# Layer 3's softmax sums as block sums on VectorE in seven of eight images, image 6's output products by halves between image 7's units, and the next image's residual sums behind the last transpose

## The chip, the cores and the metric

The kernel runs on one core of one Trainium2 chip. Its time is the device time of one execution in microseconds (us). Engines: TensorE (PE) multiplies matrices, VectorE (DVE) and ScalarE (ACT) work on elements, GpSimd (POOL) does some additions, SyncE (SP) issues most DMAs. Each engine takes its instructions in a fixed order and waits at an instruction until its operands are there.

## The reference

Eight images of 384 channels and 32 x 32 positions pass four residual layers, x = x + layer(normalised x): layer 0 an attention with convolved queries, keys and values, layer 1 a mixture of four experts per position, layer 2 a 3 x 3 depthwise and a 1 x 1 convolution with ternary weights, layer 3 an attention with keys and values sampled at 256 learned points. All is float32. The change is in the end of layer 3:

```
attn = jax.nn.softmax(jnp.einsum('bhqd,bhkd->bhqk', qh, k) * SCALE, axis=-1)   # 6 heads, 1024 queries, 256 keys, 64 wide
out = jnp.einsum('bhqk,bhkd->bhqd', attn, v)
out = out.transpose(0, 1, 3, 2).reshape(B, DIM, H, W)
out = jnp.einsum('bchw,oc->bohw', out, proj_w) + proj_b[None, :, None, None]
```

## The kernel before

A tile holds one image as 128 partitions x 3 chunks x 1024 positions. Layers 0 and the first pass of layer 1 fill the first half of the time. After that a loop goes over the images: the generator `layers(b)` gives layers 2 and 3 of image b in small steps, and between two steps units of layer 1 of image b + 1 (`layer1`, its matmuls into `ph` at L1492 and `y` at L1513) are put in, so that PE has work while DVE does the convolution of layer 2 (`y<-h,tap,y`, L1632). From this a scheduler makes one fixed order for each engine. Image 7 has no image after it: `last_image` takes what is left of image 6's generator by `fill(n)`, n steps at a time, and puts it between its own steps.

`attend` is the attention of layer 3. It has six units u, one for each pair of heads pr (0 to 2) and half of the queries h (0, 1). A unit is:

- scores: four matmuls into two tiles `s`, each of the two-bank tag `big`, of which there are two (L1867);
- ACT takes the exponentials of both into two tiles `p` (L1884), and POOL adds the two into `p01` (L1953);
- four matmuls of `p` with the values into `pav`, of a bank of its own (L1893), which DVE transposes by 32 x 32 blocks into `tu` (L1965);
- the sum of the exponentials over the keys, in one of two ways. `sums` (L1906): two matmuls of `ones` with `p01` into `pss`, 64 columns of PE each, and DVE transposes the 128 x 512 result into `ts` (L1938). Or `block_sums` and `join`: DVE transposes `p01` by blocks (`tp`, L1917, 128 x 1024) and adds over each block's 32 (`bsum`, L1919), and two matmuls with 16 columns of operand add up the partitions into `pbs` (L1926);
- `divide`, one unit later: DVE takes the reciprocal (L1935 or L1939), multiplies `tu` by it (L1940) and transposes into the slice of `att` that belongs to pr and h (L1943).

`blocks` says how many units take the second way: units 0 to 3 of images 0 to 5, none of images 6 and 7. After the units come the output products: for each of three row blocks m, six matmuls `pf<-att,wp` into one `big` tile (halves h, and pr within a half, L2022), and DVE adds bias and x (L2030) and a DMA takes the result out.

`layer1(b + 1)` begins with `attended`: three DVE instructions `x<-o,bnsc_out,x` of 128 x 1024 (L1226), one for each chunk, then ACT's `h` (L1442), which the first `ph` needs. In the order of before they stand on DVE among the divisions of image b's units 4 and 5. After the output products the two small matmuls `gna_d` and `gnb_d` (L117, L128) give the norm with which layer 2 of the next image starts.

Of the kernel before, what the change touches and what calls it, by code (L numbers as in the profile page):

```python
# [9 lines left out]
ALU = mybir.AluOpType  # L10
AX = mybir.AxisListType

B, C, H, W = 8, 384, 32, 32
N = H * W
P = 128
# [40 lines left out]
def tile_kernel(ctx: ExitStack, tc: tile.TileContext, i: dict, out: bass.AP):  # L56
# [1344 lines left out]

    x2_dram = dram.tile([B, P, KC, N], F32, name="x2")
    om_dram = dram.tile([B, 3, NG * LS], F32, name="omd")
    NU3, NB3 = 2 * NPAIR3, 4
    rec3 = wd.tile([P, B * NU3, 16], F32, name="rec3")
    bad3 = wd.tile([P, 1], mybir.dt.int32, name="bad3")

# [7 lines left out]
    def layer1(pl, b, late=False):  # L1415
# [13 lines left out]
        def enter(h):  # L1429
            hs = slice(h * HALF, (h + 1) * HALF)  # L1430
            if late and h == 1:

                h1 = [pl.one([P, HALF], t, f"h1_{b}_{t}", n) for t, n in (("cb", 2), ("w0", 1))]
                h1.insert(0, pl.one([P, HALF], "cb", f"h1_{b}", 2))
            else:
                h1 = pl.one([P, KC, HALF], "h1", f"h1_{b}_{h}")
                h1 = [h1[:, c, :] for c in range(KC)]
            state["h1"] = h1
            if h == 0 and not late:
                attended(xt, ots)  # L1440
            for c in range(KC):
                nc.scalar.activation(  # L1442
                    h1[c], xt[:, c, hs], AF.Identity,
                    bias=sb1[:, b, c : c + 1], scale=rs1[:, b : b + 1],
                )
# [385 lines left out]
    def attend(pl, b, xt, put, general, q, xs, fill=nothing):  # L1831
# [69 lines left out]
        if not general:  # L1901
            def sums(u, p01):

                pss = fbank(f"pss3_{b}_{u}")
                for j in range(2):
                    nc.tensor.matmul(  # L1906
                        pss[64 * j : 64 * j + 64, :], lhsT=ones[:, :64],
                        rhs=p01[:, j * HALF : (j + 1) * HALF], start=True, stop=True,
                    )
                return pss  # L1910

            blocks = NB3 if b < B - 2 else 0

            def block_sums(u, p01):

                t = pl.one([P, 32, 32], "ts", f"tp_{b}_{u}")
                nc.vector.transpose(t.rearrange("p a b -> p (a b)"), p01)  # L1917
                bsum = small.tile([P, 32], F32, tag="bsum", name=f"bsum_{b}_{u}")
                nc.vector.reduce_sum(bsum, t, AX.X)  # L1919
                return bsum  # L1920

            def join(u, bsum):

                pss = fbank(f"pbs3_{b}_{u}")
                for j in range(2):
                    nc.tensor.matmul(  # L1926
                        pss[64 * j : 64 * j + 64, :16], lhsT=same,
                        rhs=bsum[:, 16 * j : 16 * j + 16], start=True, stop=True,
                    )
                return pss  # L1930

            def divide(pss, pr, h, u, tu):
                rc = rec3[:, b * NU3 + u, :]
                if u < blocks:
                    nc.vector.reciprocal(rc, pss[:, :16])  # L1935
                else:
                    tss = pl.one([P, 16, 32], "ts", f"ts_{b}_{u}")
                    nc.vector.transpose(tss.rearrange("p a b -> p (a b)"), pss)  # L1938
                    nc.vector.reciprocal(rc, tss[:, :, 0])  # L1939
                nc.vector.tensor_tensor(  # L1940
                    tu, tu, rc.unsqueeze(2).to_broadcast([P, 16, 32]), ALU.mult
                )
                nc.vector.transpose(  # L1943
                    att[:, pr, h * HALF : (h + 1) * HALF], tu.rearrange("p a b -> p (a b)")
                )


            ps, due3 = exps(0, scores(*units[0])), None
            fill(1)
            yield UNIT  # L1950
            for u, (pr, h) in enumerate(units):
                p01 = pl.flat([P, N], f"p01_{b}_{u}")
                nc.gpsimd.tensor_tensor(p01, ps[0], ps[1], ALU.add)  # L1953
                nxt = scores(*units[u + 1]) if u + 1 < NU3 else None
                if last and nxt:
                    nxt = exps(u + 1, nxt)
                pav = weigh(pr, h, ps)
                if due3:
                    pss = (join if due3[2] < blocks else sums)(due3[2], due3[4])
                if nxt:  # L1960
                    ps = nxt if last else exps(u + 1, nxt)

                tu = pl.one([P, NG * LS], f"om{u % 2}", f"tu_{b}_{u}")[:, :HALF]
                tu = tu.rearrange("p (a b) -> p a b", b=32)
                nc.vector.transpose(tu.rearrange("p a b -> p (a b)"), pav)  # L1965
                if due3:
                    divide(pss, *due3[:4])
                due3 = pr, h, u, tu, block_sums(u, p01) if u < blocks else p01
                if u < KC:
                    fill(1)  # L1970
                yield UNIT
                yield 0.0
            divide(sums(due3[2], due3[4]), *due3[:4])
            yield 3.0
        else:
            for pr, h in units:
                pav = vbank(f"pav3_{b}_{pr}_{h}")
                for j in range(2):
                    r = slice(64 * j, 64 * j + 64)
                    nm = f"3_{b}_{pr}_{h}_{j}"  # L1980
                    s = big(f"s{nm}").rearrange("p (a k) -> p a k", a=4)
                    for qc in range(4):
                        q0 = h * HALF + qc * P
                        nc.tensor.matmul(
                            s[:, qc, :], lhsT=q[r, pr, q0 : q0 + P], rhs=kt[r, pr, :],
                            start=True, stop=True,
                        )
                    mx = small.tile([P, 4], F32, tag="mx4", name=f"mx{nm}")
                    nc.vector.reduce_max(mx, s, AX.X, negate=True)
                    nc.vector.tensor_scalar(mx, mx, 0.125, None, ALU.mult)  # L1990
                    p = pl.flat([P, 4, LS], f"p{nm}")
                    rs = small.tile([P, 4], F32, tag="rs4", name=f"rs{nm}")
                    for qc in range(4):
                        nc.scalar.activation(
                            p[:, qc, :], s[:, qc, :], AF.Exp, bias=mx[:, qc : qc + 1],
                            scale=0.125, accum_out=rs[:, qc : qc + 1],
                        )
                    nc.vector.reciprocal(rs, rs)
                    nc.vector.tensor_tensor(
                        p, p, rs.unsqueeze(2).to_broadcast([P, 4, LS]), ALU.mult  # L2000
                    )
                    pt = pl.flat([P, 2, HALF], f"pt{nm}")
                    for kc in range(2):
                        tp = fbank(f"tp{nm}_{kc}")
                        for qc in range(4):
                            nc.tensor.transpose(
                                tp[:, qc * P : (qc + 1) * P], p[:, qc, kc * P : (kc + 1) * P], ident
                            )
                        nc.vector.tensor_copy(pt[:, kc, :], tp)
                    hd = 2 * pr + j  # L2010
                    for kc in range(2):
                        nc.tensor.matmul(
                            pav[r, :], lhsT=vt[:, kc, hd * 64 : (hd + 1) * 64], rhs=pt[:, kc, :],
                            start=(kc == 0), stop=(kc == 1),
                        )
                nc.vector.tensor_copy(att[:, pr, h * HALF : (h + 1) * HALF], pav)
        for m in range(KC):
            pf = big(f"pf_{b}_{m}")
            for h in range(2):
                hs = slice(h * HALF, (h + 1) * HALF)  # L2020
                for pr in range(NPAIR3):
                    nc.tensor.matmul(  # L2022
                        pf[:, hs], lhsT=wp3[:, pr, m * P : (m + 1) * P], rhs=att[:, pr, hs],
                        start=(pr == 0), stop=(pr == NPAIR3 - 1),
                    )

            n = 2 if last and m == KC - 1 else 1
            for k in range(n):
                ks = slice(k * N // n, (k + 1) * N // n)
                nc.vector.scalar_tensor_tensor(  # L2030
                    xt[:, m, ks], pf[:, ks], pb3[:, m : m + 1], xt[:, m, ks], ALU.add, ALU.add
                )
                put(m, xt, ks)
            yield 0.0

    oks = wd.tile([P, 2], F32, name="oks")
# [138 lines left out]
    with pd:  # L2175
# [30 lines left out]
        def fill(n):  # L2206
            for _ in range(n):
                next(this, None)
# [173 lines left out]
```

## Time and profile before

| what | value |
|---|---|
| median of 3 runs | 3445.78 us (3443.03 to 3448.07) |
| the profiled execution | 3446.12 us, span of its trace 3444.3 us |
| granted clock of PE | 0.99 |
| PE, DVE, ACT, POOL busy | 97%, 51%, 38%, 6% of the span |
| DMA over the span | 68 GB/s in the mean |

The span runs from the first to the last instruction; the execution is 1.8 us longer. A float32 matmul stands in the trace as two records, so 36 records of `pf` are 18 matmuls.

### The profile page before, as it was taken

The page shows a single profiled execution, that of the slowest core. Times are in us where ns is not written, and L with a number is a line of the kernel's source. Part 1 is how long each engine was busy: PE and PEld are TensorE (multiplying, and loading weights), DVE is VectorE, ACT ScalarE, POOL GpSimd, SP SyncE. Part 2 cuts the span into 40 slices and gives each one's busy share as a digit, 9 for nine tenths or more (in the row PEclk, how much of TensorE's full clock was granted, in tenths as well). Part 3 has the DMA queues.
Part 4 walks back from the last instruction along what each step waited for, and adds up shares of the span by engine and source line. Part 5 has one row for each costly group of instructions (what it writes and reads, how often), then busy time and mean ns, then how long its engine had stood idle before and what let it go on. Part 6 is the DMA issues. An engine that isn't in the chain of part 4 may idle for free.

```text
span 3444.3 us, 44805 instructions
## 1 busy us (share of the span) xinstructions
PE 3338.8 (97%) x18479; PEld 1445.0 (42%) x18479; DVE 1754.6 (51%) x2961; ACT 1300.2 (38%) x1519; POOL 203.7 (6%) x237
## 2 busy tenths in 40 slices
PE   6989999999999999998889999999999999999988
PEld 2433434343434343433334444444444444444443
DVE  8952232323232323234456575565755657548764
ACT  5655444444444444433212323223232232322341
POOL 2100000000000000000000100101001010020121
PEclk9999999999999999999999999999999999999999
DMA  9973121212121212021810110101101001010000
GB/s 354 295 222 80 27 80 27 80 27 80 26 81 26 80 27 79 28 75 44 309 35 22 36 46 30 55 22 36 42 33 55 22 36 40 36 55 22 0 19 38
DMA packets 86547, 234.56 MB, mean 68 GB/s; under 512 B 21832, under 2 KB 22056, under 8 KB 79418
## 3 DMA queue, kind: packets, MB, share of 16 engines
q1 hardware_dynamic: 84170, 223.30, 20.1%
q10 hardware_dynamic: 1248, 4.72, 0.4%
q8 instruction: 149, 2.44, 0.3%
q0 software_dynamic: 912, 3.53, 0.3%
q14 instruction: 68, 0.56, 0.1%
HBM read 146.33 MB, written 75.59 MB: 64 GB/s over the span
## 4 chain that ended last, share of the span: by engine, by line
PE 43%; DVE 7%; ACT 1%; DMA 1%; POOL 0%; issue 0%; SPq 0%; DVEq 0%; POOLq 0%; ACTq 0%
PE y L1513 12%; PE ph L1492 11%; DVE y L1632 4%; PE pf L2022 4%; PE pq L1673 3%; PE pw L1644 3%; PE pav L1893 3%; PE s L1867 2%; PE pk L1838 1%; DVE hd L1478 1%; DVE off L1769 1%; PE pv L1849 1%; PE pss L1906 1%; PE xsb L1819 1%; PE pw_last L2071 1%; PE xs L1819 0%
## 5 line engine op out<-in xcount | busy, mean ns | idle before, releaser
L827 ACT ACTIVATE p<-s 128x1024 f32<-128x1024 f32 x512 | 496.3, 1021 | 365.7 <-PE s L820 365.5
L1492 PE MATMUL ph<-h,w_sb 128*128 128x512 f32 x1104 | 487.2, 596 | 14.7 <-DMA b_sb<-in_b_dram 14.5
L1513 PE MATMUL y<-hd,w_sb 128*128 128x512 f32 x1080 | 487.2, 599 | 10.8 <-DVE hd L1478 10.8
L835 PE MATMUL pav<-p,vt 64*64 64x512 f32 x4096 | 494.8, 589 | 0.0
L820 PE MATMUL s<-qk,qk 48*64 48x512 f32 x2944 | 355.2, 592 | 0.0
L1492 PEld LDWEIGHTS ph<-h,w_sb 128*128 128x128 f32 x1104 | 208.1, 191 | 272.0 <-issue 265.4
L1513 PEld LDWEIGHTS y<-hd,w_sb 128*128 128x128 f32 x1080 | 200.0, 191 | 242.1 <-issue 220.3
L796 DVE COPY ta<-pav 128x512 f32<-128x512 f32 (+1 forms) x65 | 44.2, 681 | 475.2 <-PE pav L835 475.2
L835 PEld LDWEIGHTS pav<-p,vt 64*64 64x64 f32 x4096 | 168.4, 133 | 273.6 <-issue 273.3
L1502 ACT ACTIVATE hd<-ph,b_sb 128x512 f32<-128x512 f32 x180 | 122.7, 682 | 308.4 <-PE ph L1492 308.4
L574 PE MATMUL pk<-xs,cws_sb 32*32 32x496 f32 (+3 forms) x3840 | 179.3, 605 | 40.5 <-DMA xs<-in_xs_dram 24.6
L1769 DVE SCALAR_TENSOR_TENSOR off<-q,dw_sb,off 128x225 f32<-128x225 f32 (+4 forms) x441 | 215.3, 542 | 2.6
L1632 DVE SCALAR_TENSOR_TENSOR y<-h,tap,y 128x961 f32<-128x961 f32 (+1 forms) x168 | 202.8, 1227 | 0.5
L820 PEld LDWEIGHTS s<-qk,qk 48*64 48x64 f32 x2944 | 109.4, 133 | 211.2 <-issue 190.3
L81 DVE COPY qk<-pq 128x512 f32<-128x512 f32 x46 | 31.8, 691 | 251.9 <-PE pq L258 251.9
L1884 ACT ACTIVATE p<-s 128x1024 f32<-128x1024 f32 x96 | 93.7, 1021 | 170.8 <-PE s L1867 161.4
L1478 DVE TENSOR_TENSOR hd<-hd,cb 128x512 f32<-128x512 f32 x180 | 122.2, 684 | 37.7 <-ACT hd L1502 37.5
L574 PEld LDWEIGHTS pk<-xs,cws_sb 32*32 32x32 f32 (+1 forms) x3840 | 80.3, 111 | 137.9 <-issue 49.2
L1953 POOL TENSOR_TENSOR p<-p,p 128x1024 f32<-128x1024 f32 x48 | 113.6, 2367 | 335.3 <-ACT p L1884 306.4
L820 PE MATMUL s<-ql,ql 48*64 48x512 f32 x1024 | 128.3, 592 | 0.2 <-ACT p L827 0.2
L2022 PE MATMUL pf<-att,wp_sb 128*128 128x512 f32 x288 | 127.4, 596 | 0.0
L711 PE MATMUL pv<-wv_sb,g 128*128 128x384 f32 x384 | 127.1, 489 | 0.0
(369 smaller groups left out, 3748.6 us busy)
## 6 DMA issues: line engine op xcount, KB each, us to landing
rqk<-y SPq DMA_DIRECT2D x96, 256.0 KB
g<-rqk SPq DMA_DIRECT2D x96, 256.0 KB
xs<-in_xs_dram SPq DMA_DIRECT2D x56, 384.0 KB
g<-rv SPq DMA_DIRECT2D x48, 256.0 KB
xh<-in_x_dram SPq DMA_DIRECT2D x48, 256.0 KB
f<-in_x_dram SPq DMA_DIRECT2D x24, 512.0 KB
f<-o SPq DMA_DIRECT2D x24, 512.0 KB
o<-ot SPq DMA_DIRECT2D x42, 256.0 KB
```

Source lines behind the costliest of these rows:

```text
L574: nc.tensor.matmul(banks[r][cols[q]].rearrange("p (h w) -> p h w", w=W)[:, :, c0:c1], lhsT=cws[rs, c, 2 * h + g, x, w], rhs=src[rs, :, c0 ...
L711: nc.tensor.matmul(pv[:, :C], lhsT=acts[b][2][:, c, t * P : (t + 1) * P], rhs=w_in[2][:, c, :], start=(c == 0), stop=(c == KC - 1),)
L820: nc.tensor.matmul(s[64 * k : 64 * k + 64, j * HALF : (j + 1) * HALF], lhsT=kt[r, k0 : k0 + 64], rhs=qt[r, h * HALF : (h + 1) * HALF], sta ...
L827: nc.scalar.activation(p, s, AF.Exp, scale=scale)
L835: nc.tensor.matmul(pav[k][64 * j : 64 * j + 64, :], lhsT=vts[b % 2][r, kc, 2 * hd : 2 * hd + 2, :].rearrange("p a b -> p (a b)"), rhs=p[r, ...
L1478: nc.vector.tensor_tensor(hd, hd, state["cb"], ALU.mult)
L1492: ahead["ph"] = nc.tensor.matmul(ph, lhsT=w1[:, e, c, dc * P : (dc + 1) * P], rhs=state["h1"][c], start=(c == 0), stop=(c == KC - 1),)
L1502: nc.scalar.activation(hd, ph, AF.Relu, bias=b1[:, k : k + 1])
L1513: nc.tensor.matmul(y, lhsT=w2[:, e, dc, m * P : (m + 1) * P], rhs=state[h, k], start=(k == 0), stop=(k == NE * KC - 1),)
L1632: nc.vector.scalar_tensor_tensor(d, f, tap2[:, c, t : t + 1], d, ALU.mult, ALU.add)
L1769: nc.vector.scalar_tensor_tensor(d, f, dw3[:, t : t + 1], d, ALU.mult, ALU.add)
L2022: nc.tensor.matmul(pf[:, hs], lhsT=wp3[:, pr, m * P : (m + 1) * P], rhs=att[:, pr, hs], start=(pr == 0), stop=(pr == NPAIR3 - 1),)
```

## The change

Images 0 to 5 and 7 take block sums for all six units (`joined = b != B - 2`); image 6 keeps the matmuls with `ones` for all of its units. Image 6's output products go by halves: three matmuls into one bank of the tag `f` (three banks, shared with the small sums), an addition of 128 x 512 and a DMA for each half, and a step of the generator behind each; `last_image` calls `fill(1)` in every one of image 7's units, not in the first three alone. `attended` of the next image is issued after the last transpose into `att`.

```diff
-    NU3, NB3 = 2 * NPAIR3, 4
+    NU3 = 2 * NPAIR3
...
             if h == 0 and not late:
-                attended(xt, ots)
+                with tc.issue_after(ahead["att"].ins) if "att" in ahead else nullcontext():
+                    attended(xt, ots)
...
-            blocks = NB3 if b < B - 2 else 0
+            joined = b != B - 2
...
-                if u < blocks:
+                if joined:
                     nc.vector.reciprocal(rc, pss[:, :16])
...
-                nc.vector.transpose(
+                ahead["att"] = nc.vector.transpose(
                     att[:, pr, h * HALF : (h + 1) * HALF], tu.rearrange("p a b -> p (a b)")
                 )
...
-                    pss = (join if due3[2] < blocks else sums)(due3[2], due3[4])
+                    pss = (join if joined else sums)(due3[2], due3[4])
...
-                due3 = pr, h, u, tu, block_sums(u, p01) if u < blocks else p01
-                if u < KC:
-                    fill(1)
+                due3 = pr, h, u, tu, block_sums(u, p01) if joined else p01
+                fill(1)
                 yield UNIT
                 yield 0.0
-            divide(sums(due3[2], due3[4]), *due3[:4])
+            divide((join if joined else sums)(due3[2], due3[4]), *due3[:4])
...
+        halves = [slice(h * HALF, (h + 1) * HALF) for h in range(2)]
+
+        def output(pf, m, hs):
+
+            for pr in range(NPAIR3):
+                nc.tensor.matmul(
+                    pf, lhsT=wp3[:, pr, m * P : (m + 1) * P], rhs=att[:, pr, hs],
+                    start=(pr == 0), stop=(pr == NPAIR3 - 1),
+                )
+
+        def add(pf, m, ks):
+            nc.vector.scalar_tensor_tensor(
+                xt[:, m, ks], pf, pb3[:, m : m + 1], xt[:, m, ks], ALU.add, ALU.add
+            )
+            put(m, xt, ks)
+
         for m in range(KC):
+            if b == B - 2:
+                for h, hs in enumerate(halves):
+                    pf = fbank(f"pf_{b}_{m}_{h}")
+                    output(pf, m, hs)
+                    add(pf, m, hs)
+                    yield 0.0
+                continue
             pf = big(f"pf_{b}_{m}")
...
+            for hs in halves:
+                output(pf[:, hs], m, hs)
+            for ks in halves if last and m == KC - 1 else [slice(0, N)]:
+                add(pf[:, ks], m, ks)
             yield 0.0
```

What the schedulers make of it, in each engine's order. On PE, at the end of images 0 to 5: `pav` of unit 4, `pbs` of units 3 and 4, one matmul of `pf`, `pav` of unit 5, five of `pf`, `pbs` of unit 5, six of `pf`, one of the next image's `ph`, six of `pf`, two of `ph`, `gna_d`. On DVE there: `tu` of unit 4, both reciprocals, both products, both transposes into `att`, `tu`, `tp` and `bsum` of unit 5, its division, two of the three sums of `attended`, two of `x<-pf`, then the third sum. On PE in image 7: in each unit three matmuls of image 6's `pf` where six stood in units 0 to 2, and `pbs` where `pss` stood. On SP the one difference is that image 6 goes out in six DMAs of 256 KB, not three of 512 KB.

More of the change, by code (lines that the diff above doesn't have):

```diff
@@ L2016, in attend @@
                 nc.vector.tensor_copy(att[:, pr, h * HALF : (h + 1) * HALF], pav)
-        for m in range(KC):
-            pf = big(f"pf_{b}_{m}")
[L2019 to L2033, printed above, removed]
+        halves = [slice(h * HALF, (h + 1) * HALF) for h in range(2)]
[10 more added lines that the diff above has]
+            put(m, xt, ks)
+        for m in range(KC):
+            if b == B - 2:
[5 more added lines that the diff above has]
+                continue
+            pf = big(f"pf_{b}_{m}")
+            for hs in halves:
+                output(pf[:, hs], m, hs)
+            for ks in halves if last and m == KC - 1 else [slice(0, N)]:
+                add(pf[:, ks], m, ks)
             yield 0.0
```

## The prediction

> **What bounds the kernel.** First the page's busy times:
>
> ```profile
> PE 3338.8 (97%) x18479; PEld 1445.0 (42%) x18479; DVE 1754.6 (51%) x2961; ACT 1300.2 (38%) x1519; POOL 203.7 (6%) x237
> ```
>
> PE hardly ever stands, at a granted clock of 0.99, so what counts is PE's own work and the waits that PE meets. Next the chain of waits at a junction, the end of image 4's attention:
>
> ```profile
> 2854.11 1.87 PE pav L1893 x8
> 2855.98 0.07 PE pbs L1926 x4
> 2856.06 0.89 PE pss L1906 x2
> 2856.95 1.88 PE pav L1893 x8
> 2858.83 1.72 PE pss L1906 x6
> 2860.55 3.63 PE pf L2022 x8
> 2864.18 1.72 PE ph L1492 x4
> 2865.89 12.02 PE pf L2022 x28
> 2877.91 0.86 PE ph L1492 x2
> 2878.77 0.12 PE gna_d L117 x2
> ```
>
> It is PE alone, piece upon piece, for 24.66 us (2854.11 to 2878.77): DVE ends nothing here, and the windows give it 16.89 us busy of 25.00, so it has room. Then the chain of waits in image 7's units:
>
> ```profile
> 3380.87 5.36 PE pf L2022 x12
> 3386.23 0.03 issue
> 3386.26 1.29 DVE x L2030
> 3387.55 0.04 issue
> 3387.60 1.13 PE s L1867 x4
> 3388.73 1.87 PE pav L1893 x8
> 3390.59 0.86 PE pss L1906 x4
> 3391.45 5.36 PE pf L2022 x12
> ```
>
> Here DVE is in the chain: `pf` holds one of the two `big` tiles until DVE has emptied it, and the second half of the scores stands behind that. Such a unit takes 10.58 us (3380.87 to 3391.45), three times. Last, PE's timeline in an ordinary unit of image 4:
>
> ```profile
> 2838.86 1.99 PE L1867 MATMUL s<-q,kt 64*128 64x512 f32 x8
> 2840.78 1.94 PE L1893 MATMUL pav<-p,vt 128*64 128x512 f32 x8
> 2842.55 0.24 PE L1926 MATMUL pbs<-bsum,same_sb 128*64 128x16 f32 x4
> 2842.72 2.84 PE L1513 MATMUL y<-hd,w_sb 128*128 128x512 f32 x6
> ```
>
> By starts: s 1.92, pav 1.77, pbs 0.17, three full matmuls 2.77, in all 6.63 (the next s starts at 2845.49). This is the form that image 7's units get.
>
> **Prices.** A full matmul (two records) is 12.02 / 28 x 2 = 0.86 us. Two matmuls of 64 columns run side by side: `pav`'s four take 1.72, a pair of `pss` 0.86. Three full matmuls take 2.77, not 2.57, before PE turns to another tile shape: a change of shape costs about 0.2. `pbs` adds only 0.07 behind `pav`, whose shape it has.
>
> The Trainium skill, "TensorEngine Tiling (Array Packing)", under Key Properties, says that changing the tiling mode drains the engine, and gives no time. It speaks against the new order, and the 0.2 per change agrees that there is a price; were changes free, a junction would save 0.8 more.
>
> **Junctions of images 0 to 5, PE.** Removed: `pss` of units 4 and 5, 0.89 + 1.72 = 2.61. Added: `pbs` of unit 4 0.07, of unit 5 about 0.1, alone among full matmuls. The order after goes pav, pbs, one pf, pav, five pf, pbs, pf: five changes of shape at 0.2 = 1.0, where before there was one (in the 3.63 of eight records, 3.43 of work). The 18 `pf` (15.45) and three `ph` (2.58) stay. Sum after: pav 1.87 + 1.72, pbs 0.24, pf 15.45, ph 2.58, changes 1.0, and 0.2 of waiting (next paragraph): 23.06. Against 24.66 that is 1.6 less; ends: 1.0 if a change in this place costs 0.3, 2.4 if changes cost nothing and nothing waits. I take 1.6, since the 0.2 is read in every unit.
>
> **Junctions, DVE.** Unit 4's transpose of `p01` (1.25) and sum (1.20) fall mostly into the wait of 1.93 before `tu` of unit 4, and both `ts` (0.71 each) go. Counted from the start of unit 4's `pav`, with DVE's rows: `tu` of unit 4 from +2.0 to +2.7; two reciprocals to +3.0; the product for unit 3 meets POOL's addition for unit 5 (+1.4 to +3.7) and takes 1.41 as at 2856.92 in the trace, not 0.65; second product and both transposes to +6.1; `tu`, `tp`, `bsum` of unit 5 (0.72 + 1.25 + 1.20, each overlapped by its follower by 0.08) to +9.1. PE comes to `pbs` of unit 5 after pav 1.87, pbs 0.14, one pf and two changes 1.26, pav 1.72, a change 0.2, five pf 4.29 and a change 0.2: +9.7. The cover is 0.6 less the way from DVE to PE; as it is thin I count 0.2 of waiting. Then reciprocal, product, transpose (0.22 + 0.65 + 0.70) to +11.8, while PE has three `pf` (2.6) that need none of it.
>
> The Trainium skill, "SBUF — State Buffer", in "SBUF: two separate sides", calls the port that DVE and GpSimd share an exclusive lock that an instruction of two SBUF operands waits for; 1.41 against 0.65 agrees, and without it the cover would be 1.4 and the 0.2 nothing.
>
> **The held sums.** `x<-o` starts behind that transpose (+11.8 to +13.1), ACT's `h` needs 0.81 more (+13.9), PE asks for it at the first `ph` at about +15.2: cover 1.3. The third sum stands behind two `x<-pf` of 1.28; its `h` is there at +19.8, its `ph` comes at +22: cover 2. The six last `pf` need the first `x<-pf` to free a `big` tile: +15.6 against +16, the thinnest cover, 0.4. The loads of `o` leave SP at 2856.06 to 2859.24 (+2 to +5), when tiles of units 4 and 5 come free, and the second has landed at 2862.43 (+8.3; DVE waited 0.60 for it): behind the hold they are no longer waited for. So the hold costs nothing, and 1.3 us of lateness on DVE would be free in it. `gnb_d` moves one `ph` (0.86) towards `gna_d`, so the convolution starts with that much more room; PE waited there 0.17 (the timeline's `pw` at 2922.30), so I count nothing. Six junctions: 6 x 1.6 = 9.6 us.
>
> **Image 7.** Before, from image 6's first `pf` to image 7's first `pf`: 3380.87 to 3420.97 = 40.10. After: four units of the form above, 4 x 6.63 = 26.5; then three `pf` 2.77, pav 1.87, pbs 0.07, three `pf` 2.77 and the last `pbs` with its changes 0.4, in all 34.4. Saved 5.7: it contains six `pss` pairs (5.2 of PE) and the three waits for `big` (0.3 each), less the extra changes. DVE in such a unit: 0.72 + 0.22 + 1.25 + 0.65 + 1.21 + 0.70 + 0.71 (half a `pf`, at the row of L1519's 128x512) = 5.5 of 6.63, in a line behind POOL's 2.35; `tu` of the next unit is met with 0.5 to spare. `tp` of unit 0 gets in front of image 6's last transpose, which the first `pf` half doesn't need. Taken 5.3, with ends of 4.5 and 6.5. After 3420.97 all stays: 18 `pf`, two sums, the last DMA. The six smaller DMAs leave once per unit; the last of them has over 15 us until the end.
>
> **Sum.** 3446.12 for the profiled execution, less 9.6 and 5.3: 3431.2; the median lies 0.34 below that execution: 3431.
>
> **Rivals.**
> *Slower: the held sums become the bound.* On DVE, after unit 5's long division, `x<-o`, `h`, `ph` are one line, and PE's order has that `ph` in front of six `pf`. For: three DVE products in this stretch may be hit by POOL (one took 2.02 at 3378.17), and DVE's share rises from 16.9 to over 20 of 23 us. Lateness d beyond the walk costs PE d at `pbs` of unit 5 or at `ph`; above 1.6 a junction loses. At d = 4.0: 6 x 2.4 - 5.3 = +9.1, 3455. It decides from d = 2.5 (6 x 0.9 = 5.3). Against: two hits of POOL at 0.7 to 1.4 make 2.7 at most. Chance 0.05.
> *Only the tail pays.* Changes of shape at 0.4 and a wait of 0.8 eat the junctions' 1.6: 3446.1 - 5.3 = 3441. Chance 0.07.
> *More at each junction.* Changes cheaper than 0.2, because some of them lie in latency that was there, and DVE's earlier convolution takes away PE's short stands at `pw` (0.3 by the starts 2920.25 and 2922.30): 2.4 x 6 + 5.7 = 20, 3426. Chance 0.15.
> *The forecast:* 0.73.
>
> **Numbers.** A measurement of this kernel tells about 0.2%, 6.9 us, from no change. The forecast's own ends are 6 x 1.0 + 4.5 = 10.5 and 6 x 2.4 + 6.5 = 20.9, so 3425 to 3436; up to 3440 it takes in most of the tail-only case. Forecast and third rival are faster by over 0.2%: 0.88; tail-only is within: 0.07; slower 0.05.
>
> **What would show it.** Right: the junction from unit 4's `pav` to `gna_d` at 23.0 instead of 24.66, with a wait under 0.5 before `pbs` of unit 5 and none before `ph`; no `pss` left but image 6's; image 7's units at 6.6 to 6.8 and no wait of `s` for `x` L2030; `pf` of image 6 to `pf` of image 7 near 34.8. Wrong: a wait of over 1 us for `bsum` or `att` at each junction; units of image 7 set by DVE at over 7.5; or a longer stand at `pw`.

## The result

The kernel after takes 3426.51 us (median of 6 runs, 3423.38 to 3429.08). The kernel before, run beside it on the same chip, takes 3446.45 us (3443.03 to 3449.01). The ratio is 0.9941, 95% interval 0.993 to 0.9952: faster, by about 20 us. The profiled execution of after took 3426.77 us with a span of 3424.7, at a granted clock of 0.989 (before: 3446.12, 3444.3 and 0.990).

The page's busy times, after:

```profile
PE 3325.3 (97%) x18479; PEld 1440.2 (42%) x18479; DVE 1776.0 (52%) x2982; ACT 1300.0 (38%) x1519; POOL 203.7 (6%) x237
```

PE has 13.5 us less to do and DVE 21.4 more, and PE still carries the span. Where the span's 19.6 us went is read stage by stage. The chain of waits at image 4's junction, after (start, duration, engine, what, line, records):

```profile
2844.30 1.87 PE pav L1894 x8
2846.17 0.19 PE pbs L1927 x8
2846.36 1.06 PE pf L2022 x2
2847.41 1.87 PE pav L1894 x8
2849.28 4.49 PE pf L2022 x10
2853.77 0.23 PE pbs L1927 x4
2854.00 5.35 PE pf L2022 x12
2859.34 0.86 PE ph L1493 x2
2860.20 5.15 PE pf L2022 x12
2865.35 1.72 PE ph L1493 x4
2867.07 0.12 PE gna_d L117 x2
```

From unit 4's `pav` to `gna_d` it is 22.77 us (2844.30 to 2867.07) where it was 24.66. It is PE alone again: no wait at `pbs` of unit 5 and none at `ph`. The `pss` are gone, and short pieces with more changes of tile shape between them stand in their place.

PE's timeline in image 7's units, after (start, time, engine, line, operation, shapes, records; a bracket behind a row would be a wait):

```profile
3367.01 2.84 PE L2022 MATMUL pf<-att,wp_sb 128*128 128x512 f32 x6
3369.78 1.99 PE L1868 MATMUL s<-q,kt 64*128 64x512 f32 x8
3371.70 1.94 PE L1894 MATMUL pav<-p,vt 128*64 128x512 f32 x8
3373.47 0.24 PE L1927 MATMUL pbs<-bsum,same_sb 128*64 128x16 f32 x4
3373.64 2.84 PE L2022 MATMUL pf<-att,wp_sb 128*128 128x512 f32 x6
...
3401.25 1.98 PE L2022 MATMUL pf<-att,wp_sb 128*128 128x512 f32 x4
```

A unit is 6.63 us (3367.01 to 3373.64), with no wait of `s` for `x`. From image 6's first `pf` to image 7's first it is 34.24 (3367.01 to 3401.25), where it was 40.10.

The third place lies 42 us behind each junction, where layer 2's last products begin. PE's timeline there, first of before, then of after:

```profile
2920.25 1.88 PE L1644 MATMUL pw<-y,upw 128*128 128x512 f32 x4
2922.30 14.00 PE L1644 MATMUL pw<-y,upw 128*128 128x512 f32 x32 [0.17 <-DVE y L1632]
```

```profile
2908.55 15.61 PE L1645 MATMUL pw<-y,upw 128*128 128x512 f32 x36
```

Before, PE stood after four records until DVE had the last `y`, and its first record after the stand is longer; after, it runs through. The whole is best read as distances between starts on PE's timeline (the chain dates its pieces a little differently, so its junctions are 0.1 longer). These hardly differ from image to image (before 24.56 to 24.65 in the first column, after 22.67 or 22.68), much less than whole executions do. The second column is from `pw` to the `gna_d` behind it, which is layer 3's norm, in images 1 to 5 (image 6 has other work there, and its 23.18 is the same in both); the third is from image 6's first `pf` to PE's last matmul.

| kernel | unit 4's pav to next gna_d | pw to next gna_d | first pf of image 6 to end |
|---|---|---|---|
| before | 24.56 | 19.32 | 55.94 |
| after | 22.67 | 18.88 | 50.07 |

The sum: 11.5 us in six junctions, 5 x 0.44 = 2.2 at `pw`, 5.9 in image 7. That is 19.6, the difference of the two spans; outside these stretches a start that is 0.4 earlier and other stretches that are 0.3 longer all but cancel.

### The profile page after: what moved, and what is told of

It is laid out like the page before. It is cut to its first block, busy times and chain, and to the rows that moved or that the text cites. A ratio compares the mean times of both kernels' runs of the same rounds, so it can differ in the third digit from the quotient of the medians.

```text
span 3424.7 us, 44837 instructions
## 1 busy us (share of the span) xinstructions
PE 3325.3 (97%) x18479; PEld 1440.2 (42%) x18479; DVE 1776.0 (52%) x2982; ACT 1300.0 (38%) x1519; POOL 203.7 (6%) x237
## 4 chain that ended last, share of the span: by engine, by line
PE 49%; DVE 1%; DMA 1%; ACT 0%; POOL 0%; issue 0%; SPq 0%; DVEq 0%; POOLq 0%; ACTq 0%
PE ph L1493 15%; PE y L1514 14%; PE pf L2022 4%; PE pq L1674 3%; PE pw L1645 3%; PE pav L1894 3%; PE s L1868 2%; PE pk L1839 1%; DVE off L1770 1%; PE pv L1850 1%; PE xsb L1820 1%; PE pw_last L2083 1%; PE xs L1820 0%; PE px L1734 0%; PE plog L1239 0%; PE pom L1701 0%
## 5 line engine op out<-in xcount | busy, mean ns | idle before, releaser
L820 PE MATMUL s<-qk,qk 48*64 48x512 f32 x2944 | 355.2, 592 | 0.0
L820 PEld LDWEIGHTS s<-qk,qk 48*64 48x64 f32 x2944 | 109.4, 133 | 211.2 <-issue 190.3
L820 PE MATMUL s<-ql,ql 48*64 48x512 f32 x1024 | 128.2, 592 | 0.2 <-ACT p L827 0.2
```

The source lines that it names most:

```text
L820: nc.tensor.matmul(s[64 * k : 64 * k + 64, j * HALF : (j + 1) * HALF], lhsT=kt[r, k0 : k0 + 64], rhs=qt[r, h * HALF : (h + 1) * HALF], sta ...
```

## The experiments

Each kernel changes what the diff shows and nothing else; the times of before beside them are 3445.22, 3445.24 and 3445.25 us. Because the start of a run alone moves by up to 6 us from kernel to kernel (last section), the verdicts rest on the three distances above, and the times stand beside them.

### The junctions alone, and the tail alone

Images 6 and 7 as before:

```diff
-            joined = b != B - 2
+            joined = b < B - 2
...
-                fill(1)
+                if u < KC:
+                    fill(1)
...
-            if b == B - 2:
+            if False:
                 for h, hs in enumerate(halves):
```

> Images 0 to 5 as in the kernel after (block sums of all six units, held sums); images 6 and 7 as in the kernel before. Theory (the parts add): each junction takes 22.8 us from unit 4's pav to gna_d as in the kernel after, PE's stand at pw stays gone (0.44 in each of five images), image 7's stretch is back at 40.1 us. Time: 6 x 1.9 + 2.2 = 13.6 us less than before, about 3433. Rival A (the junctions' gain comes from the tail's early work or hangs on it): junctions give under 1.5 us each, 3437 or more. Rival B (the stand at pw does not hang on the junction's new order): pw to gna_d back at 19.3 us, 3435.

Measured: 22.67, 18.88 and 55.94; 3432.51 us, ratio 0.9963 (0.995 to 0.9977). Then the other half, images 0 to 5 as before:

```diff
+            joint = (lambda u: joined and (u < 4 or b == B - 1))
...
-                with tc.issue_after(ahead["att"].ins) if "att" in ahead else nullcontext():
-                    attended(xt, ots)
+                attended(xt, ots)
```

with `joint(u)` in the place of `joined` where a unit's sum is chosen.

> Images 0 to 5 as in the kernel before (four block units, pss for two, sums not held); images 6 and 7 as in the kernel after. Theory (the parts add): junctions 24.7 us, pw stand of 0.2 to 0.4 back, from image 6's first pf to image 7's first pf 34.2 us instead of 40.1; time 5.9 us less than before, about 3440.5. Rival (the tail is faster only because image 5 hands over earlier, or the tail pays less than its PE work): stretch over 35.5 us, 3442 or more.

Measured: 24.56 to 24.81, 19.32 and 50.07; 3440.5 us, ratio 0.9986 (0.9977 to 0.9995). By the distances the parts add: 13.7 and 5.9 us of 19.6. By the medians they give 12.7 and 4.7. The rivals fall: the junctions give 1.9 us each without the tail's change, the stand at `pw` goes with them, and the tail gives its whole 5.9 without theirs.

### Without the hold, and the hold alone

```diff
-                with tc.issue_after(ahead["att"].ins) if "att" in ahead else nullcontext():
-                    attended(xt, ots)
+                attended(xt, ots)
```

> The kernel after without the held sums: x<-o goes back between the parts of unit 5's division on DVE, and the program's order moves two ph ahead of the last slice of the first pf and gnb_d back to its old distance from gna_d. Theory: unit 5's att is ready about 3.7 us later, the two ph (1.7) and a cover of 0.8 take part of it, PE waits about 1.2 for att at each junction, which takes 23.5 to 24.5 us instead of 22.8, and PE's stand at pw (0.44 per image) comes back, as gnb_d is later: 6 x 1.2 + 2.2, 3433 to 3439. Rival A (the hold is worth nothing, the block sums do it all): junction 22.8, pw without stand, 3426.5. Rival B (without the hold the block sums lose all they gain): junction 24.7 or more, 3440 or more.

Measured: 22.67, 19.71; 3430.16 us, ratio 0.9959 (0.9945 to 0.9973). I had the place wrong. The junction loses nothing: unit 5's last transpose ends 2.9 us later than in the kernel after, counted from unit 4's `pav`, but the program's order has put two `ph` in front of the `pf` that need it. What is lost stands at `pw`, in PE's timeline of this kernel:

```profile
2909.71 1.88 PE L1644 MATMUL pw<-y,upw 128*128 128x512 f32 x4
2912.15 14.00 PE L1644 MATMUL pw<-y,upw 128*128 128x512 f32 x32 [0.56 <-DVE y L1632]
```

The reverse: the kernel before with the hold, and nothing else of the change. It is the first experiment's kernel with two units by `pss` in images 0 to 5:

```diff
+            joint = (lambda u: joined and u < 4)
```

> The kernel before with the held sums alone (four block units, pss for two, image 7 as before). The order on PE has the three ph behind all pf and gnb_d one ph (0.86) nearer to gna_d. Theory (the hold pays 42 us later, at pw, and nowhere else): junction 24.56 from unit 4's pav to gna_d as in the kernel before, pw to gna_d 18.88 instead of 19.32 us in five images, 5 x 0.44 = 2.2 us less than before, about 3443. Rival A (the hold pays only together with the block sums): pw to gna_d stays at 19.32, no change. Rival B (the hold shortens the junction too, since unit 5's att comes earlier): junction under 24.0, 3440 or less.

Measured: 24.56, 18.88 and 55.94; 3442.53 us, ratio 0.9991 (0.9982 to 1.0), as the theory had it. The four together (junction / `pw` to `gna_d`):

| | sums not held | sums held |
|---|---|---|
| `pss` for units 4 and 5 | 24.56 / 19.32 | 24.56 / 18.88 |
| block sums | 22.67 / 19.71 | 22.67 / 18.88 |

The block sums take 1.89 from a junction with or without the hold. The hold takes nothing from it, but 0.44 at `pw` by itself and 0.83 when the block sums have come, since these by themselves push `gnb_d` one `ph` further back. What counts for the second number is PE's way from `gnb_d` to `pw`. It is 40.54 us with the hold, and PE does not stand; 39.68 in the kernel before, and it stands 0.44; 38.82 with the block sums and no hold, and it stands 0.83. These are one, two and three `ph` between `gna_d` and `gnb_d`. The convolution of layer 2 on DVE starts from `gnb_d`; its last `y` ends 0.45 before PE asks for it in the kernel after, so the first `ph` of 0.86 costs 0.4. The next costs only 0.4 too; in that kernel's trace one addition of 0.69 (`hd<-hd,cb`) stands on DVE ahead of the norm and not behind it, which may account for the rest, but this was not tried by itself.

### The two parts of the tail

Halves, but image 7's sums by `pss`:

```diff
-            joined = b != B - 2
+            joined = b < B - 2
```

> The kernel after, with image 7's sums by pss on PE instead of on DVE; image 6's output products by halves as in the kernel after. Theory (each part of the tail pays for itself): each unit has pss 0.86 instead of pbs 0.17, so 6.63 + 0.7 = 7.3 us, and from image 6's first pf to image 7's first pf 34.24 + 6 x 0.7 = 38.4 us, of which the halves alone gave 1.7; time 4.2 us over the kernel after, about 3430.7. Rival (the halves do it all, pss lying in time in which PE waits for DVE): 34.5, 3426.8. Rival (the halves alone give nothing, as the pss make up for it): 40, 3432.4.

Measured: 22.67, 18.88; 38.94 us between the two first `pf` and 54.77 to the end; 3431.74 us, ratio 0.9954 (0.994 to 0.9967). A unit in the chain of waits:

```profile
3375.29 2.77 PE pf L2022 x6
3378.07 1.92 PE s L1868 x8
3379.98 1.87 PE pav L1894 x8
3381.85 0.86 PE pss L1907 x4
3382.71 2.77 PE pf L2022 x6
```

7.42 us, PE alone; `pss` costs the 0.79 that it is longer than `pbs`, not the 0.7 that I had put down. The other half, block sums with image 6's products whole:

```diff
-                fill(1)
+                if u < KC:
+                    fill(1)
...
-            if b == B - 2:
+            if False:
```

> The kernel after, with image 6's output products whole behind units 0 to 2 of image 7 as in the kernel before; image 7's sums on DVE. Some of image 7's own products get between its last units, so the measure is from image 6's first pf to the end of PE's work: 55.9 us in the kernel before, 50.1 in the kernel after. Theory (each part of the tail pays for itself): the loop pf 5.36, x 1.29, s 1.13, pav 1.87 loses only its pss (0.86, pbs 0.07 in its place), three units of 9.8, and the three later ones save 0.7 each: 4.1 less than before, 51.8 us, time 1.7 over the kernel after, about 3428.2. Rival (the wait for big grows, since DVE has bsum's 2.45 to do beside x): 53.5 us or more, 3430 or more. Rival (the halves are worth nothing once the pss are gone): 50.1, 3426.5.

Measured: 52.82 to the end; 3429.27 us, ratio 0.9949 (0.9936 to 0.9963). The first three units are 9.80 and 9.80 apart as worked out, and the one us that I missed is in the later ones, which have no `pf` of image 6 between them. PE's timeline there:

```profile
3393.54 1.13 PE L1868 MATMUL s<-q,kt 64*128 64x512 f32 x4 [0.32 <-DVE x L2029]
...
3398.46 1.94 PE L1894 MATMUL pav<-p,vt 128*64 128x512 f32 x8
3400.23 0.24 PE L1927 MATMUL pbs<-bsum,same_sb 128*64 128x16 f32 x4
3401.27 0.29 PE L1927 MATMUL pbs<-bsum,same_sb 128*64 128x16 f32 x4 [0.80 <-DVE bsum L1920]
```

The bracket of 0.80 is PE waiting for `bsum`: the block sums need DVE's 2.4 us per unit, and without work between the units PE is there first. So the parts of the tail do not add. The halves alone give 1.2 us (55.94 to 54.77), the block sums alone 3.1 (to 52.82), both 5.9 (to 50.07). The halves are worth 2.7 once the `pss` are gone: they end the three waits for `big`, and they give each unit three matmuls that cover DVE's sums. By the starts, the scores with the bracket of 0.32 take 2.51 us instead of 1.92, so each of the three waits costs 0.59, and the wait for `bsum` costs 1.0 (1.26 us for the `pbs` of two units, of which 0.24 is work); together that is 2.8. The halves alone give less, since each of their three further pairs of shape changes costs 0.19: 1.77 less 0.57 is 1.2.

### Lateness on DVE

Three transposes into a tile that nobody reads, around unit 5's last transpose:

```diff
+                if u == NU3 - 1 and b < B - 2:
+                    t2 = pl.one([P, 32, 32], "ts", f"late_{b}").rearrange("p a b -> p (a b)")
+                    for k in range(3):
+                        nc.vector.transpose(
+                            t2[:, :HALF], tu.rearrange("p a b -> p (a b)")
+                        )
                 ahead["att"] = nc.vector.transpose(
                     att[:, pr, h * HALF : (h + 1) * HALF], tu.rearrange("p a b -> p (a b)")
```

> The kernel after with three extra transposes of 128x512 on DVE (0.7 us each, 2.1 us in all) around unit 5's last transpose in each of six junctions, into a tile that nobody reads; PE's order is that of the kernel after, on DVE the second x<-o goes behind two x<-pf. Theory (the held sums have cover): the first x<-o comes 1.4 later against a cover of 1.5 for its ph, the first x<-pf 0.9 later against 0.9 for the third pf, DVE's gap of 1.5 before the last x<-pf takes most of the rest: junction 22.7 to 22.9, 3426.5 to 3428. Rival (the held sums stand on the brink, each us of lateness costs one): 0.7 to 1.4 per junction, 3430.7 to 3435.

Measured: 22.71, 18.88, 50.07; 3426.97 us, ratio 0.9943 (0.9929 to 0.9956). Two us of idle work behind unit 5's product cost 0.04. The scheduler has put the first held sum between the idle transposes, so that it starts 1.2 us later than in the kernel after, not 2.1. DVE's timeline:

```profile
2855.62 0.71 DVE L1947 STREAM_TRANSPOSE late<-tu 128x512 f32<-128x512 f32 x1
2856.26 0.67 DVE L1950 STREAM_TRANSPOSE att<-tu 128x512 f32<-128x512 f32 x1
2856.85 0.67 DVE L1947 STREAM_TRANSPOSE late<-tu 128x512 f32<-128x512 f32 x1
2857.44 1.24 DVE L1226 SCALAR_TENSOR_TENSOR x<-o,bnsc_out,x 128x1024 f32<-128x1024 f32 x1
2858.60 0.71 DVE L1947 STREAM_TRANSPOSE late<-tu 128x512 f32<-128x512 f32 x1
...
2865.99 1.28 DVE L2034 SCALAR_TENSOR_TENSOR x<-pf,pb_sb,x 128x1024 f32<-128x1024 f32 x1
2867.82 0.16 DVE L119 COPY ga_d<-gna_d 128x2 f32<-128x2 f32 x1 [0.55 <-PE gna_d L117]
```

The wait of 1.55 that DVE has before the last `x<-pf` in the kernel after is gone, and the wait for `gna_d` is the same 0.55: the lateness is used up before the norm.

Lateness further ahead, before `bsum` of unit 5 (the transpose of `p01` done twice, then three times):

```diff
-                nc.vector.transpose(t.rearrange("p a b -> p (a b)"), p01)
+                for k in range(2 if u == NU3 - 1 and b < B - 2 else 1):
+                    nc.vector.transpose(t.rearrange("p a b -> p (a b)"), p01)
```

> The kernel after with unit 5's transpose of p01 done twice (1.25 us more on DVE ahead of bsum of unit 5) in each of six junctions. The program's order answers on PE: one more pf ahead of pbs of unit 5, gnb_d one ph later. Measured from unit 4's pav to gna_d and on to the next gna_d. Theory (lateness ahead of bsum is covered by the moved pf, and paid 42 us later): cover 0.5 + 0.86 against 1.25, junction 22.7; pw to gna_d 18.88 + 0.44, as gnb_d comes one ph later: 5 x 0.44 over the kernel after, about 3428.7. Rival (the cover at pbs of unit 5 was 0.5 and the rest is waited for): 0.75 per junction, 23.4, 3431 to 3433.

Measured: 22.71, 19.33; 3430.01 us, ratio 0.9958 (0.9942 to 0.9975). As the theory had it: the junction doesn't see 1.25 us of lateness, and the second `ph` between the two norm matmuls costs 0.45 at `pw`, as it costs 0.44 in the kernel before.

> The kernel after with unit 5's transpose of p01 done three times (2.5 us more on DVE ahead of bsum of unit 5) in each of six junctions. The program's order on PE has three more pf ahead of pbs of unit 5 and gna_d in front of the pf that need unit 5's att. Measured from unit 4's pav to pw, 64.32 us in the kernel after. Theory (pbs is covered by 0.5 + 2.6, but att then has one pf and gna_d as its cover, 1.0 against 2.0 from pbs to att): a wait of 1.0 per junction, 65.3 us, about 6 over the kernel after, 3432.5. Rival A (the order takes it all): 64.3, 3426.5. Rival B (lateness beyond the first cover of 0.5 is paid in full): 1.9 to 2.0 per junction, 66.2, 3438.

With `3 if` in the place of `2 if`, measured: 65.65 us from unit 4's `pav` to `pw`, against 64.32, so 1.3 more per junction; 18.88 from `pw` to `gna_d`; 3434.42 us, ratio 0.9968 (0.9956 to 0.9981). PE's timeline shows where it is paid:

```profile
2861.99 0.29 PE L1928 MATMUL pbs<-bsum,same_sb 128*64 128x16 f32 x4
2862.22 1.12 PE L2023 MATMUL pf<-att,wp_sb 128*128 128x512 f32 x2
2863.18 0.28 PE L117 MATMUL gna_d<-mv_d,g_sb 128*128 128x2 f32 x2
2864.33 1.98 PE L2023 MATMUL pf<-att,wp_sb 128*128 128x512 f32 x4 [0.87 <-DVE att L1945]
```

`pbs` does not wait; with only one `pf` left between it and the `pf` that need unit 5's slice of `att`, that division is waited for. I had 1.0, the trace has 0.87 in the bracket, 1.0 by the starts (1.15 from `gna_d` to that `pf`, less 0.14 for `gna_d`), and some longer records behind the wait. Three `ph` stand between `gna_d` and `gnb_d` here, and yet PE does not stand at `pw`: `gna_d` has moved ahead, and the way from `gnb_d` to `pw` is 41.40.

### Block sums for image 6 too

```diff
-            joined = b != B - 2
+            joined = True
```

> The kernel after with block sums on DVE for image 6 too (units in the two convolution-free stages beside image 7's convolution); no pss anywhere. Theory: PE saves 6 pairs of pss there (up to 5 us), but in that stretch DVE has 0.72 + 0.22 + 1.25 + 0.65 + 1.21 + 0.70 per unit beside the convolution of image 7 and becomes the bound: the transpose of p01 and the sum are 2.45 per unit against 1.4 (transpose of ts and sum of pss) before; the stretch gets 0 to 6 us longer, 3427 to 3433. Rival (DVE has room there as in the junctions): 2 to 5 us less than the kernel after, 3422 to 3425.

Measured: 22.67, 18.88, 50.07; 3426.78 us, ratio 0.9948 (0.9934 to 0.9961), the same as the kernel after as far as can be told. From layer 3's `gna_d` of image 6 to its first `pf` it is 217.0 us against 216.5. The windows over the end of that stretch, after, then this kernel (span of the window, then busy us and instructions of PE, PEld, DVE, ACT, POOL, clock, DMA):

```profile
3301.89:3367.01 65.12, 57.16 (x221) 26.54 (x219) 41.44 (x61) 26.61 (x40) 21.45 (x16) 0.87 0.00 0
```

```profile
3304.97:3370.68 65.71, 51.98 (x220) 24.07 (x218) 47.92 (x68) 26.52 (x40) 21.16 (x16) 0.90 0.00 0
```

PE does 5.2 us less and DVE 6.5 more, and the stretch is no shorter. The half us by which it is longer tells nothing: in the eleven other kernels, whose order on PE is the same there, this stretch takes between 215.4 and 217.3 us. PE has waits there to begin with (57.16 of 65.12 us busy), so its saved work is worth nothing. That DVE becomes the bound is not shown; it is busy for 47.92 of 65.71. No experiment gave a kernel faster than after.

## Why the prediction was right, step by step

The forecast was 3431.0 with a range of 3425 to 3440; 3426.51 is inside it, 4.5 below the number. Three terms make them up: 1.9 us at the six junctions together, 2.2 at `pw` and 0.6 in image 7.

**Junctions, PE's sum (9.6 forecast, 11.5 measured).** The sum of pieces holds. The five changes of shape, read off the chain above, are 0.20 (1.06 - 0.86), 0.15 (1.87 - 1.72), 0.20 (4.49 - 4.29), 0.16 (0.23 - 0.07) and 0.20 (5.35 - 5.15): 0.91, where I had 1.0. The Trainium skill, "TensorEngine Tiling (Array Packing)", under Key Properties, says that a change of tiling mode drains the engine; these five agree that a change has a price, which is small here. The mis-sized term is the 0.2 of waiting at `pbs` of unit 5, which did not come. `bsum` of unit 5 ends 8.96 after unit 4's `pav` (forecast 9.1), PE comes at 9.47 (forecast 9.7); the cover of 0.5 was enough in each of six images. I had put a wait there only because the cover was thin. DVE came a little early, as the product beside POOL's addition took 1.12, not 1.41. One end of the range doesn't follow from its own terms: with no price for changes and no wait, 1.2 us go from the sum of 23.06, which makes 2.8 per junction and not 2.4; the range would then begin near 3423.

**The stand at `pw` (counted as nothing, 2.2 measured).** This is the step that failed. I read the bracket of 0.17 in the timeline, saw that `gnb_d` comes 0.86 nearer, and then put nothing down. The stand's true length was 0.44: the distance of the starts over the stand was 2.05 for 1.72 of work, and the first record behind it takes 0.70, not 0.59. It occurs in five images. The hold alone (18.88 against 19.32) and the 1.25 us of lateness (19.33 again) show that it hangs on the place of `gnb_d`. The forecast's range has no term for it; the 2.2 us fitted into the room that was left for cheaper changes of shape.

**"The hold costs nothing"** was right and too little: the 2 x 2 table shows that the hold is worth 0.83 in each of five images, 4.2 us of the 20, all of it at `pw`. The cover that I had worked out for the first held sum, 1.3 us, is borne out as far as it was tried: 1.2 us of lateness cost 0.04.

**Image 7 (5.3 forecast, 5.86 measured).** The working gave 34.4 us from `pf` to `pf`, the trace 34.24. I took 5.3 instead of its 5.7 for caution, with no row behind it; that is the error. The two sources of the saving that I named, the `pss` and the waits for `big`, were the right ones, but the waits were read too short: 0.3 each by the bracket, 0.59 by the starts. And the edits behind them do not simply add: the two experiments on the tail show 1.2 and 3.1 alone and 5.9 together.

**The rivals.** *More at each junction* named 3426, and its number is nearer than the forecast's, in part by luck. Its part on `pw` was right; its other part, changes of shape that are clearly cheaper than 0.2, was not: 0.91 of 1.0 was paid. The wait that did not come, which it did not name, stands for the rest. *Only the tail pays* falls with the first experiment (the junctions alone give 12.7 us). *The held sums become the bound* did not come about: `bsum` of unit 5 ended at 8.96, ahead of the walk's 9.1. Its price is only half tested. At 2.5 us of lateness, put in as further transposes, the junction loses 1.3 and not 2.5, so it keeps 0.6 of its gain; but there the program's order knew of the lateness and moved `pf` ahead. Lateness that the order doesn't know of, such as the hits of POOL that the rival named, was not tried, nor was a lateness of 4.

## What to carry to other kernels

Where PE is the bound, a sum of its pieces from timeline rows, changes of shape included, was good to 0.1 us in 23; put no wait on top where the walk shows a cover, even a thin one (0.5 us was enough here), and no discount because a working feels large. Follow every instruction that an edit moves to the next place where that chain is waited for, even 40 us later, count how often that place occurs, and take a stand's length from the starts on both sides, not from the bracket alone. And two edits may be worth more together than apart: try each alone before saying which one pays.

## What the runs showed of the hardware that was not expected

The time up to layer 3's first attention, where these kernels' orders on PE do not differ yet, is not steady: unit 0's first `pav` of image 0 starts between 1961.35 and 1967.39 us in the profiled executions. The three distances used here repeat to 0.1 us in nearly all images and kernels. The runs show how much of the 5 or 6 us by which executions of one kernel scatter lies ahead of that point: each kernel's median less the distance from that `pav` to the end of its profiled span is 1965.9 to 1966.9 us in all twelve kernels, so in these executions it is nearly all. By that distance the junctions alone give 13.6 us, the tail alone 5.7 and both 19.2. Most of the scatter arises early: the first score matmul of layer 0 (`s`, L820) starts between 235.57 and 240.30 us, this spread of 4.7 is still the same at 1600 us, and it is 6.0 at that `pav`. A difference of 2 us, which the times can hardly tell, is plain in the distances. What moves the start remains open.
